# Splitting the first loads of a fused mean, matmul and residual kernel over three DMA queues

## The chip, the core and the metric

The kernel runs on one core of one Trainium2 chip. Its time is the device time of one execution in microseconds (us); lower is better. A core has TensorE (PE; its weight loads are shown as PEld), VectorE (DVE), ScalarE (ACT), GpSimd (POOL) and SyncE (SP), each with an instruction stream of its own that it works off in order, and 16 DMA engines that move data between the chip's main memory and the on-chip memory. A transfer is started by an instruction in the stream of SP, ACT or POOL; we call the transfers that one engine starts that engine's queue.

## The reference

Cut to what is computed (x is 4 x 1024 x 512, cond_512 is 4 x 256, W is 1536 x 512, b has 512 elements, all float32):

```python
hidden = jnp.concatenate([cond_512, cond_512], axis=-1)
x_mean = jnp.mean(x, axis=1, keepdims=True)
fused = jnp.concatenate([x, x_mean * ones_L, hidden[:, None, :] * ones_L], axis=-1)
out = x + jax.nn.relu(jnp.einsum('bld,do->blo', fused, W) + b)
```

The last two thirds of `fused` are the same for all 1024 positions of a row, so the kernel computes them once for each of the 4 rows as a bias: W's middle block times the mean of x, W's last block times cond (its two halves added first, since both halves of `hidden` are the same), plus b. What is left for every position is x times W's first block, plus that bias, then relu, then x is added again.

## The kernel before

**Tiles.** x is cut into 32 tiles `t` of 128 positions, 8 for each row. A tile's product needs x transposed, in 4 pieces `j` of 128 input columns, against `w_x[:, j]`, the rows of W's first block that belong to j. Float32 accuracy comes from a split: each operand is divided into a rounded part (`hi`, `w_hi`) and a remainder (`lo`, `w_lo`), and a product is three matmuls, hi by w_hi, hi by w_lo and lo by w_hi (`product`, line 576). So a tile is 12 matmuls of 128 x 512, and the 32 tiles are 384 of them.

**Steps for a piece.** `turn` (378) transposes: tiles 0 to 5 on TensorE by matmuls with an identity (389), later ones on VectorE from a second copy `z` of x that was loaded in another layout (391). `split_hi` (410) rounds on ScalarE, `split_lo` (429) subtracts, mostly on VectorE. Tiles 0 and 1 are turned whole, four transposes each; from tile 2 on, two tiles are turned together, one j at a time. The PSUM pool of the transposes has two buffers, so the turn of a piece waits until the `split_lo` of the piece two before it has read its buffer.

**The bias.** `fill` (396) transposes cond on TensorE (`pw`, from `c_sb`) and issues two matmuls on constants behind that. `turn_cond` (472) makes, on VectorE, `bL` from `b_sb` (473) and `cT` from `pw` (474); further steps on ScalarE, GpSimd and VectorE build `biases[r]`.

**Order.** The kernel does not write its order out by hand. `Plan` (20) holds every step with a cost on each engine that may do it, the steps it needs, and a due time. `simulate` and `run` try 1500 variations of the priorities with a fixed random seed, and the best simulated schedule is then emitted step by step. What an engine gets is therefore a fixed sequence. On the chip an engine waits at the head of its sequence until the data is there; nothing is reordered then. The times in the plan (`plan.done[...] = (at - HANDOVER, ...)`) are guesses that the planner takes for granted: when a load will have landed, or, with `later=3.0`, how long after its issue.

**The start, which the change touches.** Lines 226 to 244 run before the plan: a small activation that makes ScalarE load its function table (`table_warm`, 229), the identity, 9 matmuls on constants (`N_WARM`, 234), and on GpSimd the memsets of `b_sb` and of the mean matrix. Line 295 loads cond into `c_sb` over ScalarE's queue. Then lines 296 to 306 start seven loads, all over SyncE's queue in this order: x tile 0, x tile 1, W piece 0, W piece 1, W pieces 2 and 3, x tiles 2 and 3, x tiles 4 and 5. `load_mean` (319) follows; everything else is started by the plan. Two steps matter later: the load of `b_sb` (406) stands in ScalarE's sequence behind the rounding of the W pieces (it needs `("w_hi", J - 1)` in the plan), and `fill` (408) stands, in the plan, behind `("turn", 1)`, the transposes of tile 1:

```python
plan.add(("b",), {"act": 0.25}, [("w_hi", J - 1)], FIRST + 4, lambda e: nc.scalar.dma_start(
    out=b_sb[0:1, :], in_=b.rearrange("(o d) -> o d", o=1)), later=3.0)
plan.add(("fill",), {"pe": 0.22 * N_FILL + 0.2}, [("turn", 1)], 5.8, lambda e: fill())
```

Of the kernel before, what the change touches and what calls it, by code (L numbers as in the profile page):

```python
# [9 lines left out]
F32 = mybir.dt.float32  # L10
F32R = mybir.dt.float32r
BF16 = mybir.dt.bfloat16
AF = mybir.ActivationFunctionType
# [140 lines left out]
def kernel(  # L154
# [22 lines left out]
    nc = tc.nc  # L177
    B, L, D = x.shape
    H = cond.shape[1]
    P = 128  # L180
# [9 lines left out]
    N_FIRST = 1  # L190
# [12 lines left out]
    N_FILL = 2  # L203

    const = ctx.enter_context(tc.tile_pool(name="const", bufs=1))
# [11 lines left out]
    plan = Plan(["pe", "dve", "act", "pool", "sp", "aq"])  # L217
# [8 lines left out]
    warm = nc.const_aps.tensor(1.0, [P, 512], BF16)  # L226
    ones = const.tile([P, 1], F32, name="ones")
    nc.vector.memset(ones, 1.0)
    table_warm = const.tile([P, 1], F32, name="table_warm")
    nc.scalar.activation(table_warm, ones, AF.Relu)  # L230
    ident = const.tile([P, P], F32, name="ident")
    make_identity(nc, ident)
    pw = ps_b.tile([P, 512], F32, tag="b", name="pw")
# [4 lines left out]
    c_sb = const.tile([B, H], F32, name="c_sb")  # L238
# [28 lines left out]
    def load_x(e, g, i=0, n=G):  # L267
        r, k = divmod(g * G, NK)
        if not i:
            xs[g] = xpool.tile([P, G, D], F32, tag="x", name=f"x{g}")  # L270
        e.dma_start(out=xs[g][:, i : i + n], in_=xv[r, :, k + i : k + i + n, :])  # L271
# [17 lines left out]
    SP = 0.72  # L289
    SPZ2 = 1.85  # L290
    SPZ = 1.3
    def load_w(e, j, n):
        e.dma_start(out=w_x[:, j : j + n, :], in_=Wv[0, :, j : j + n])  # L293

    nc.scalar.dma_start(out=c_sb, in_=cond)
    for key, at, e, load in (
        (("x", 0, 0), 4.4, nc.sync, lambda e: load_x(e, 0, 0, 1)),
        (("x", 0, 1), 5.0, nc.sync, lambda e: load_x(e, 0, 1, 1)),
        (("w", 0), 5.8, nc.sync, lambda e: load_w(e, 0, 1)),
        (("w", 1), 7.0, nc.sync, lambda e: load_w(e, 1, 1)),  # L300
        (("w", 2), 8.4, nc.sync, lambda e: load_w(e, 2, 2)),
        (("x", 0, 2), 9.7, nc.sync, lambda e: load_x(e, 0, 2, 2)),
        (("x", 1, 0), 11.0, nc.sync, lambda e: load_x(e, 1, 0, 2)),
    ):
        load(e)
        plan.done[key] = (at - plan.HANDOVER, 0.0, "sp")
    w_cond = xpool.tile([P, 2, KH, D], F32, tag="x", name="w_cond")

    def load_cond():
        nc.sync.dma_start(  # L310
            out=w_cond, in_=W[2 * D : 3 * D].rearrange("(s h p) o -> p s h o", p=P, h=KH)
        )
# [3 lines left out]
    def load_mean(j, n):  # L316
        nc.sync.dma_start(out=w_mean[:, j : j + n, :], in_=Wv[1, :, j : j + n])

    load_mean(0, N_FIRST) if N_FIRST else None
    plan.free["sp"] = 8.9 + SP * N_FIRST  # L320
    plan.add("cond", {"sp": 4 * SP}, [], 13, lambda e: load_cond(), later=2.5)
    plan.add("w_mean", {"sp": (J - N_FIRST) * SP}, ["cond"], 14,
             lambda e: load_mean(N_FIRST, J - N_FIRST), later=2.5)
# [72 lines left out]
    def fill():  # L396
        for h in range(KH):
            nc.tensor.transpose(
                pw[:, h * B : (h + 1) * B], c_sb[:, h * P : (h + 1) * P], ident[:B, :B]
            )  # L400
        for _ in range(N_FILL):
            nc.tensor.matmul(
                pw[:, KH * B :], lhsT=warm[:, :P], rhs=warm[:, KH * B :], start=True, stop=True
            )

    plan.add(("b",), {"act": 0.25}, [("w_hi", J - 1)], FIRST + 4, lambda e: nc.scalar.dma_start(
        out=b_sb[0:1, :], in_=b.rearrange("(o d) -> o d", o=1)), later=3.0)
    plan.add(("fill",), {"pe": 0.22 * N_FILL + 0.2}, [("turn", 1)], 5.8, lambda e: fill())

    def split_hi(c):  # L410
        u, js = pieces[c]
# [24 lines left out]
    for c, (u, js) in enumerate(pieces):  # L436
# [12 lines left out]
        w = n * len(js)  # L449
# [273 lines left out]
```

## Time and profile before

| what | us |
|---|---|
| median of 8 executions | 108.86 |
| lowest and highest | 107.76, 109.85 |
| the profiled execution | 108.40 |
| span of the profile, first to last instruction | 106.6 |
| outside the span in that execution (108.40 - 106.6) | 1.8 |

All of the profile's times are counted from the span's start. The engines' busy times over the span:

```profile
PE 101.3 (95%) x443; PEld 79.6 (75%) x443; DVE 77.3 (73%) x118; ACT 57.6 (54%) x136; POOL 75.8 (71%) x68
```

TensorE is the busiest; its granted clock is given as 1.000 for the whole span. The 40 slices of 2.67 us show the DMA engines busy nearly throughout, and how much they moved at the start:

```profile
DMA  3999999999999999999999999999963399516552
GB/s 70 214 291 399 263 346 230 257 195 198 197 198 224 192 216 315 264 264 305 378 236 345 295 324 265 275 276 400 395 243 127 126 347 400 209 39 251 201 216 80
```

A digit is the busy share in tenths (9 is 90% or more); below it stands what was moved. The list of transfers, with the size of each and the median time from the issue to the landing (only the groups of the start):

```profile
x<-in_x_dram SPq DMA_DIRECT2D x2, 256.0 KB, 2.8
w_x<-in_L_cond_W_dram SPq DMA_DIRECT2D x2, 256.0 KB, 5.4
w_x<-in_L_cond_W_dram SPq DMA_DIRECT2D x1, 512.0 KB, 6.4
```

The first line is x tiles 0 and 1, the others are W's three loads. In these lists the suffix q (SPq, ACTq) stands for the engine's sequencer, which issues transfers and waits for semaphores while the engine itself may be busy with something else.

### The profile page before, as it was taken

Reading aid. Unit: us, or ns where it says so; the run is one execution under the profiler, and the core shown is the slowest. Engines: PE = TensorE matmul, PEld = TensorE weight load, DVE = VectorE, ACT = ScalarE, POOL = GpSimd, SP = SyncE. Lnnn points to the kernel's source line nnn. Section 1 sums busy time; section 2 is a strip of 40 time slices with the busy share of each in tenths; the row PEclk is TensorE's granted clock in tenths of the full one; section 3 lists DMA queues with packets and bytes.
Section 4 is the critical chain, followed back from the end, with each engine's and each line's share of the span. In section 5 each row is a group of like instructions: output and inputs, shape, how many; then the busy total and the mean of one; then the engine's idle time right before and its main releaser. Section 6 shows DMA issues by size and latency. Waiting matters only on the chain.

```text
span 106.6 us, 1462 instructions
## 1 busy us (share of the span) xinstructions
PE 101.3 (95%) x443; PEld 79.6 (75%) x443; DVE 77.3 (73%) x118; ACT 57.6 (54%) x136; POOL 75.8 (71%) x68
## 2 busy tenths in 40 slices
PE   7999959999999999999999999999999999999980
PEld 2547738887888878878888787888878878888870
DVE  0049643492899998999889699997998793481760
ACT  5053536595786996946597656436685520470000
POOL 5008206374499899999999989999979999099000
DMA  3999999999999999999999999999963399516552
GB/s 70 214 291 399 263 346 230 257 195 198 197 198 224 192 216 315 264 264 305 378 236 345 295 324 265 275 276 400 395 243 127 126 347 400 209 39 251 201 216 80
DMA packets 24049, 26.83 MB, mean 252 GB/s; under 512 B 1253, under 2 KB 14825, under 8 KB 24042
## 3 DMA queue, kind: packets, MB, share of 16 engines
q1 hardware_dynamic: 24032, 26.74, 92.2%
q8 instruction: 3, 0.05, 0.2%
q14 instruction: 4, 0.03, 0.1%
q10 hardware_dynamic: 10, 0.01, 0.0%
HBM read 18.36 MB, written 8.39 MB: 251 GB/s over the span
## 4 chain that ended last, share of the span: by engine, by line
PE 82%; DMA 11%; SPq 2%; DVE 1%; issue 0%; ACT 0%; DVEq 0%
PE po_None L595 77%; DMA w_x<-in_L_cond_W_dram 6%; DMA b_sb<-in_L_cond_b_dram 5%; PE po L595 3%; PE pb L521 2%; PE xT L389 1%; SPq L293 1%; SPq L271 1%; DVE bL L473 0%; DVE o L626 0%; DVE lo L432 0%; PE po L590 0%; DVE cT L474 0%; ACT w_hi L359 0%; DVEq L473 0%
## 5 line engine op out<-in xcount | busy, mean ns | idle before, releaser
L595 PE MATMUL po_None<-w_hi,hi 128*128 128x512 f32 x124 | 49.4, 400 | 0.2 <-DVE w_hi L360 0.2
L595 PE MATMUL po_None<-w_lo,hi 128*128 128x512 f32 x124 | 49.3, 399 | 0.0
L595 PE MATMUL po_None<-w_hi,lo 128*128 128x512 f32 x124 | 49.3, 399 | 0.0
L621 POOL TENSOR_TENSOR o<-o,x 128x512 f32<-128x512 f32 x28 | 35.7, 1302 | 4.2 <-ACT o L618 4.2
L416 ACT ACTIVATE hi<-xT 128x512 fp32r<-128x512 f32 (+1 forms) x38 | 20.3, 534 | 15.0 <-PE xT L389 9.8
L391 DVE STREAM_TRANSPOSE xT<-z 128x512 f32<-128x512 f32 (+1 forms) x28 | 28.1, 1031 | 0.3
L595 PEld LDWEIGHTS po_None<-w_lo,hi 128*128 128x128 f32 x124 | 23.3, 189 | 6.0 <-DVE w_lo L362 0.7
L595 PEld LDWEIGHTS po_None<-w_hi,hi 128*128 128x128 f32 x124 | 23.3, 189 | 5.9 <-ACT hi L416 0.7
L595 PEld LDWEIGHTS po_None<-w_hi,lo 128*128 128x128 f32 x124 | 23.4, 188 | 5.8 <-DVE lo L432 0.3
L432 DVE TENSOR_TENSOR lo<-xT,hi 128x512 fp32r<-128x512 f32 (+1 forms) x29 | 16.0, 575 | 4.3 <-ACT hi L416 4.3
L618 ACT ACTIVATE o<-o 128x512 f32<-128x512 f32 x28 | 16.8, 628 | 3.4 <-DVE o L613 2.5
L613 DVE TENSOR_TENSOR o<-po_None,bias 128x512 f32<-128x512 f32 x18 | 11.6, 679 | 6.1 <-issue 3.1
L613 POOL TENSOR_TENSOR o<-o,bias 128x512 f32<-128x512 f32 x10 | 13.0, 1311 | 0.5 <-ACT bias L527 0.5
L496 DVE SCALAR_TENSOR_TENSOR acc<-w_mean,tot,acc 128x512 f32<-128x512 f32 x15 | 11.3, 754 | 2.7 <-ACT acc L490 2.2
L432 POOL TENSOR_TENSOR lo<-xT,hi 128x512 fp32r<-128x512 f32 (+1 forms) x9 | 11.3, 1253 | 0.0
L507 POOL TENSOR_TENSOR cond<-bL,term 128x512 f32<-128x512 f32 x4 | 5.2, 1297 | 5.3 <-ACT term L502 5.3
L608 ACT ACTIVATE o<-po_None 128x512 f32<-128x512 f32 x10 | 5.9, 596 | 4.1 <-PE po_None L595 4.0
L362 POOL TENSOR_TENSOR w_lo<-w_x,w_hi 128x512 fp32r<-128x512 f32 x2 | 2.8, 1426 | 6.2 <-ACT w_hi L359 6.2
L416 ACT ACTIVATION_READ_ACCUMULATOR hi<-xT 128x1 f32 x36 | 7.0, 195 | 0.0
L527 ACT ACTIVATE bias<-pb 128x512 f32<-128x512 f32 x4 | 2.4, 598 | 8.2 <-PE pb L521 8.2
L389 PEld LDWEIGHTS xT<-ident,x 128*128 128x128 f32 x24 | 4.8, 209 | 2.7 <-DVE lo L432 1.7
L479 POOL TENSOR_TENSOR wc<-w_cond 128x512 f32<-128x512 f32 x2 | 2.5, 1292 | 5.7 <-DMA w_cond<-in_L_cond_W_dram 5.7
(52 smaller groups left out, 62.9 us busy)
## 6 DMA issues: line engine op xcount, KB each, us to landing
out_dram<-o SPq DMA_DIRECT2D x31, 256.0 KB, 4.0
z<-in_x_dram SPq DMA_DIRECT2D x24, 256.0 KB, 8.9
x<-in_x_dram SPq DMA_DIRECT2D x6, 1024.0 KB, 9.3
x<-in_x_dram SPq DMA_DIRECT2D x3, 512.0 KB, 8.2
w_cond<-in_L_cond_W_dram SPq DMA_DIRECT2D x1, 1024.0 KB, 10.0
w_mean<-in_L_cond_W_dram SPq DMA_DIRECT2D x1, 768.0 KB, 10.0
x<-in_x_dram SPq DMA_DIRECT2D x2, 256.0 KB, 2.8
w_x<-in_L_cond_W_dram SPq DMA_DIRECT2D x2, 256.0 KB, 5.4
```

Source lines behind the costliest of these rows:

```text
L362: lambda e, j=j: nc_of[e].tensor_tensor(w_lo[:, j, :], w_x[:, j, :], w_hi[:, j, :].bitcast(F32), ALU.subtract))
L389: nc.tensor.transpose(v[:, (m * n + i) * P : (m * n + i + 1) * P], x_t[:, j], ident)
L391: nc.vector.transpose(v[:, : n * P].rearrange("p (n t) -> p n t", t=Q), zs[u].rearrange("p n (a j) -> p n j a", j=J)[:, : n * NQ, js[0], :],)
L416: nc.scalar.activation(hi[c][:, :m], xT[c][:, :m], AF.Copy, accum_out=sums[:, r, js[0], s : s + 1] if len(js) == 1 else None,)
L432: nc_of[e].tensor_tensor(lo[c][:, :m], xT[c][:, :m], hi[c][:, :m].bitcast(F32), ALU.subtract)
L496: nc.vector.scalar_tensor_tensor(acc[r], w_mean[:, j, :], totals[r][:, j : j + 1], acc[r], ALU.mult, ALU.add)
L507: nc.gpsimd.tensor_tensor(conds[r], conds[r] if k else bL, terms[r, k], ALU.add)
L595: nc.tensor.matmul(pos[key][:, :w], lhsT=v[p][:, c], rhs=m[:, j, d], start=(not h and todo[key] == 3 * J), stop=(todo[key] == 1),)
L608: nc.scalar.activation(o_tile(t), pos[t], AF.Copy)
L613: nc_of[e].tensor_tensor(v if t >= ALONE else o_tile(t), v, biases[t // NK][:, d], ALU.add)
L618: nc.scalar.activation(outs[t], outs[t], AF.Relu)
L621: nc.gpsimd.tensor_tensor(outs[t], outs[t], x_tile(t), ALU.add)
```

## The change

The seven loads of the start keep their sizes and their helpers. The three of W go over ScalarE's queue instead of SyncE's, those of x stay on SyncE's, and the program now names them in turn. cond's load goes over GpSimd's queue; in the program it stands behind GpSimd's memsets. The activation that loads ScalarE's table stands behind the loads. In the plan, the guessed landing times change, SyncE is taken to be free at 7.8 instead of 8.9, and `fill` (cond's two transposes and the two matmuls behind them) needs only tile 0's transposes, not tile 1's. No computation is added or taken away. Since the planner works with these numbers, the order it emits for the rest of the kernel may differ as well.

```diff
@@ -226,8 +226,6 @@
     warm = nc.const_aps.tensor(1.0, [P, 512], BF16)
     ones = const.tile([P, 1], F32, name="ones")
     nc.vector.memset(ones, 1.0)
-    table_warm = const.tile([P, 1], F32, name="table_warm")
-    nc.scalar.activation(table_warm, ones, AF.Relu)
     ident = const.tile([P, P], F32, name="ident")
     make_identity(nc, ident)
     pw = ps_b.tile([P, 512], F32, tag="b", name="pw")
@@ -292,18 +290,21 @@
     def load_w(e, j, n):
         e.dma_start(out=w_x[:, j : j + n, :], in_=Wv[0, :, j : j + n])
 
-    nc.scalar.dma_start(out=c_sb, in_=cond)
+
     for key, at, e, load in (
-        (("x", 0, 0), 4.4, nc.sync, lambda e: load_x(e, 0, 0, 1)),
-        (("x", 0, 1), 5.0, nc.sync, lambda e: load_x(e, 0, 1, 1)),
-        (("w", 0), 5.8, nc.sync, lambda e: load_w(e, 0, 1)),
-        (("w", 1), 7.0, nc.sync, lambda e: load_w(e, 1, 1)),
-        (("w", 2), 8.4, nc.sync, lambda e: load_w(e, 2, 2)),
-        (("x", 0, 2), 9.7, nc.sync, lambda e: load_x(e, 0, 2, 2)),
-        (("x", 1, 0), 11.0, nc.sync, lambda e: load_x(e, 1, 0, 2)),
+        (("x", 0, 0), 4.8, nc.sync, lambda e: load_x(e, 0, 0, 1)),
+        (("w", 0), 5.1, nc.scalar, lambda e: load_w(e, 0, 1)),
+        (("x", 0, 1), 6.0, nc.sync, lambda e: load_x(e, 0, 1, 1)),
+        (("w", 1), 6.2, nc.scalar, lambda e: load_w(e, 1, 1)),
+        (("x", 0, 2), 8.3, nc.sync, lambda e: load_x(e, 0, 2, 2)),
+        (("w", 2), 8.0, nc.scalar, lambda e: load_w(e, 2, 2)),
+        (("x", 1, 0), 9.7, nc.sync, lambda e: load_x(e, 1, 0, 2)),
     ):
         load(e)
         plan.done[key] = (at - plan.HANDOVER, 0.0, "sp")
+    nc.gpsimd.dma_start(out=c_sb, in_=cond)
+    table_warm = const.tile([P, 1], F32, name="table_warm")
+    nc.scalar.activation(table_warm, ones, AF.Relu)
     w_cond = xpool.tile([P, 2, KH, D], F32, tag="x", name="w_cond")
 
     def load_cond():
@@ -317,7 +318,7 @@
         nc.sync.dma_start(out=w_mean[:, j : j + n, :], in_=Wv[1, :, j : j + n])
 
     load_mean(0, N_FIRST) if N_FIRST else None
-    plan.free["sp"] = 8.9 + SP * N_FIRST
+    plan.free["sp"] = 7.8 + SP * N_FIRST
     plan.add("cond", {"sp": 4 * SP}, [], 13, lambda e: load_cond(), later=2.5)
     plan.add("w_mean", {"sp": (J - N_FIRST) * SP}, ["cond"], 14,
              lambda e: load_mean(N_FIRST, J - N_FIRST), later=2.5)
@@ -405,7 +406,7 @@
 
     plan.add(("b",), {"act": 0.25}, [("w_hi", J - 1)], FIRST + 4, lambda e: nc.scalar.dma_start(
         out=b_sb[0:1, :], in_=b.rearrange("(o d) -> o d", o=1)), later=3.0)
-    plan.add(("fill",), {"pe": 0.22 * N_FILL + 0.2}, [("turn", 1)], 5.8, lambda e: fill())
+    plan.add(("fill",), {"pe": 0.22 * N_FILL + 0.2}, [("turn", 0)], 5.8, lambda e: fill())
 
     def split_hi(c):
         u, js = pieces[c]
```

## The prediction

> **What bounds the kernel now.** I read the page first: TensorE is busy for 95% of the span. Then I cut the span where TensorE's timeline has gaps and asked for each engine's busy time in the stretches. Columns: stretch, length, then busy time (and instructions) of PE, PEld, DVE, ACT, POOL, then granted clock, DMA share, GB/s.
>
> ```profile
> 4.50:7.42 2.92, 2.69 (x14) 1.88 (x12) 0.55 (x2) 1.19 (x2) 0.00 (x0) 1.00 0.87 222
> 7.42:9.00 1.58, 1.58 (x6) 0.87 (x7) 1.58 (x3) 0.63 (x2) 0.57 (x1) 1.00 1.00 386
> 9.00:14.47 5.47, 5.47 (x27) 4.08 (x25) 3.49 (x7) 2.70 (x10) 2.27 (x2) 1.00 1.06 329
> 14.47:15.76 1.29, 0.01 (x1) 0.01 (x1) 0.89 (x4) 0.30 (x1) 0.00 (x0) 1.00 1.06 346
> 15.76:103.60 87.84, 87.83 (x391) 71.35 (x391) 70.23 (x102) 51.30 (x121) 71.35 (x57) 1.00 0.95 255
> ```
>
> The reader is to see that from 15.76 to 103.60 TensorE never stops (87.83 of 87.84). The change takes no matmul away, so it can only move the moment at which that stretch starts, or put gaps into it. What can be had lies before: 0.23 idle before 7.42, 1.29 at 14.47, and a little between matmuls that count as busy (from 7.42 to 9.00 six matmuls fill 1.58; at the 0.233 of the later stretch, where 391 instructions include shorter ones, six take 1.40, so 0.2, and I count 0.3 with the next one). Together 1.8.
>
> Next, the chain of work that ended last (start, duration, what), for the gap at 14.47:
>
> ```profile
> 2.57 6.41 DMA w_x<-in_L_cond_W_dram
> ...
> 9.06 5.70 DMA b_sb<-in_L_cond_b_dram
> ...
> 15.37 0.34 DVE lo L432
> ...
> 15.76 0.51 PE xT L389 x2
> ```
>
> W's last load, issued at 2.57, lands at 8.97; only then does ScalarE pass its rounding of that piece and issue b's load, which takes 5.70; VectorE waits for b at `bL`, and a `lo` that TensorE's next transposes wait for is queued behind it. VectorE's own timeline shows that queue:
>
> ```profile
> 11.74 0.74 DVE L432 TENSOR_TENSOR lo<-xT,hi 128x256 fp32r<-128x256 f32 x2
> 14.87 0.43 DVE L473 TENSOR_SCALAR bL<-b_sb 128x512 f32<-128x512 f32 x1 [2.38 <-DMA b_sb<-in_L_cond_b_dram]
> 15.21 0.16 DVE L474 TENSOR_SCALAR cT<-pw 128x8 f32<-128x8 f32 x1
> 15.28 0.75 DVE L432 TENSOR_TENSOR lo<-xT,hi 128x256 fp32r<-128x256 f32 x2
> ```
>
> VectorE stands for 2.38 and TensorE, with work left for half of that, for 1.29. So not W's first piece but W's last piece, through b, sets the end. TensorE's timeline says what the first piece is worth:
>
> ```profile
> 4.50 1.91 PE L389 MATMUL xT<-ident,x 128*128 128x128 f32 x8
> 6.35 0.31 PE L398 MATMUL pw<-ident,c_sb 4*128 4x4 f32 x2
> 6.59 0.60 PE L402 MATMUL pw<-const-bfloat16-1.0 128*128 128x504 bf16 x2
> 7.42 0.71 PE L595 MATMUL po_None<-w_hi,hi 128*128 128x512 f32 x2 [0.23 <-DVE w_hi L360]
> ```
>
> The transposes of tiles 0 and 1 and `fill` occupy TensorE from 4.50 to 7.19. W's first piece holds it up for 0.23 only. Last, the DMA engines by the microsecond:
>
> ```profile
> 3.00:4.00 1.00, 1.00 (x4) 0.30 (x2) 0.00 (x0) 0.00 (x0) 0.00 (x0) 1.00 1.00 285
> 4.00:5.00 1.00, 1.00 (x5) 0.73 (x4) 0.00 (x0) 0.00 (x0) 0.00 (x0) 1.00 0.90 107
> 5.00:6.00 1.00, 1.00 (x7) 1.00 (x5) 0.00 (x0) 0.40 (x1) 0.00 (x0) 1.00 0.75 119
> 6.00:7.00 1.00, 1.00 (x6) 0.35 (x5) 0.16 (x1) 0.74 (x2) 0.00 (x0) 1.00 1.01 320
> ```
>
> They are 90% and 75% busy while they move 107 and 119 GB/s, against 386 from 7.42 on. That dip, when W's first rows are read, loses 2 x (1 - 113/386) = 1.4 us of transfer.
>
> **Part by part.** Differences are taken in the profiled execution (108.40: span 106.6 and 1.8 outside) and added to the median 108.86, which is 0.46 above it. I count the 1.8 outside as unchanged.
>
> *W on ScalarE's queue.* An issue takes 0.42 to 0.46 on SyncE (three in 1.37). First in ScalarE's sequence, W's loads are issued at about 0.73, 1.2 and 1.65 instead of 1.63, 2.09 and 2.57: 0.9 earlier each. But the first piece is worth at most 0.23 at 7.42, and an earlier w_hi and w_lo up to 0.3 between the first matmuls: -0.5 at best. For the last piece, which counts, both ends: if the dip runs beside x's loads instead of behind them, -1.4. If the queues share evenly, x tiles 2 and 3 (512 KB), which came after W, now come beside it, at 389 GB/s (the stretch from 8 to 9 us) +1.35. I take the middle, 0, since nothing in this trace shows two loaded queues at once. Here a rule of the Trainium skill speaks against the change. The row: with one queue the DMA engines are already 0.75 to 1.01 busy from 2 us on. DMA: Bandwidth & Descriptors, section "Issuing engines are not separate DMA queues", says that transfers started from several engines interleave on the same 16 DMA engines and that only issue time is saved. By it alone the sum would take the +1.35 end, less at most the 0.9 of issue; by the dip in the row, up to -1.4.
>
> *x.* Tiles 0 and 1 landed 2.8 after their issues, by 4.0; tile 0's transposes start at 4.50, when the 9 warm-up matmuls end (0.77 + 3.94, the last one's tail overlapped). Shared with W's first piece, tile 0 lands between 3.5 (as now) and 5.4 (4.0 for both pieces' 512 KB, plus the whole dip). Beyond 4.4 it costs TensorE directly: 0 to +1.0; I take +0.3, as the first half-microsecond of reading is x's as well as W's. Tile 1 may come up to 1 us later; `fill`, moved ahead of its transposes, covers 0.84 of that (6.35 to 7.19). Without that cover it would be added to the +0.3. TensorE's own path to 14.47 thus moves by -0.5 + 0.3 = -0.2, between -0.5 and +0.5.
>
> *The wait at b.* b's load is still issued behind ScalarE's rounding of W's last piece. Its 5.70 has bounds 2.8 (x's first loads) and 10.0 (`w_cond`, the longest in the list); its own row is the nearest, so 5.70. Then b lands where W's last piece puts it, VectorE's queue behind `bL` waits, and TensorE's 0.2 is swallowed there unless the planner puts another `lo` in front of `bL`. It may: the plan has x tiles 2 and 3 at 8.3 instead of 9.7 and W's first two pieces 0.7 to 0.8 earlier. One `lo` (about 0.4) more ahead of `bL` frees the next transposes. From none to the whole 1.29; I take 0.2 for the order, since the plan also moves b's own due landing ahead, by 0.4 with W's last piece.
>
> *cond on GpSimd's queue.* It stands behind memsets that end at 2.26 (1.97 + 0.29). Landing 1.7 (the fastest transfer of the list) to 5.7 (b) later: 4.0 to 8.0. TensorE needs it after tile 0's transposes, at about 5.5 (4.50 + 0.96); it used it at 6.35 before. With the 2.8 of x's loads, which ran beside the same start, it is there at 5.1: cost 0, under tile 0's transposes. At 8.0, the stall is +2.5 for everything queued behind on TensorE, tile 1's transposes first. GpSimd's next work is at 8.43, so nothing there waits for the issue.
>
> *Table load.* 1.28 plus 0.20, now from about 2.1 to 3.6; ScalarE is idle until 5.60. Cost 0; without this cover 1.5 at the first `hi`.
>
> *SyncE's other issues.* x tiles 2 to 5, `w_mean` and the first `z` leave 1.4 earlier; what they bring is first missed after 9 us. The wait for `w_cond` (GpSimd, until 16.93) has long slack before the first bias at 34.5. Cost 0 while that holds.
>
> Sum: -0.2 (order before `bL`) + 0 (W's last piece) + 0 (cond, table, SyncE) = -0.2, and 108.86 - 0.2 = 108.7.
>
> **The rivals.** *Faster: the wait at b goes.* The redrawn order puts enough `lo` ahead of `bL`, or W's last piece lands over 1 us earlier. For it: the dip of 1.4, and a plan in which x is 1.4 earlier. Against: b stays behind W. Then TensorE's -0.2 counts and the 1.29 is saved: 107.4; with every term at its best, -1.8, 107.0.
>
> *Slower: W's last piece lands later.* Place: ScalarE's rounding of it, b's issue behind, `bL` on VectorE. Price +1.35, 110.2. It decides from a landing of 10.1 on (8.97 + 1.1), if `bL` still has a `lo` behind it. For it: DMA engines that are full with one queue. Against: the dip may be hidden.
>
> *Slower: cond lands late.* `fill` ends at 8.84 instead of about 6.3, tile 1's transposes (0.96) at 9.8, the first product 2.4 later than 7.42; 1.29 of it falls into the gap at 14.47: +1.1, 110.0.
>
> *Slower: the redrawn order has a new stall.* In the 87.84 after 15.76 only 0.01 is idle, so a redraw can only lose there; one more wait like the present one is +1.3, 110.2.
>
> *No effect, because W comes no earlier:* that is the likeliest case with all terms at 0, 108.9.
>
> **How the numbers follow.** A measurement of this kernel (8 runs within 1% of the median) can't tell less than 1%, 1.09 us, from no change. Likeliest, little net: 0.38, its own range 107.8 to 109.8. The wait at b goes: 0.26. W's last piece late: 0.20. cond late: 0.08. A new stall: 0.08. So faster 0.26, same 0.38, slower 0.36. The range 107.2 to 110.4 takes in the cases at their prices and leaves out the last of each: some 0.08 below, 0.10 above.
>
> **What would show it.** In the changed profile: W's first piece landing before 6.8, but the first product no earlier than about 7.1; W's last load landing near 9, b's about 5.7 after its issue; VectorE waiting at L473 and TensorE behind it near 15. I am wrong if TensorE has no idle stretch between 9 and 17 us (then faster), if that stretch is over 2 us, if cond's transposes start after 6.5, or if TensorE idles after 17 us.

## The result, and the profile after

| | before | after |
|---|---|---|
| median (executions) | 108.87 (32) | 111.02 (11) |
| lowest and highest | 107.66, 110.13 | 110.84, 111.91 |
| the profiled execution | 108.40 | 110.87 |
| its span | 106.6 | 109.1 |
| TensorE's first product starts, last matmul ends | 7.42, 103.61 | 10.82, 105.94 |

The changed kernel is slower: after / before is 1.0243, with a 95% interval of 1.0208 to 1.0277. That is 2.3 us over the forecast and 0.6 us above the range. (Ratios here and below leave disturbed executions out, so one can differ from the quotient of two medians.)

The stretches of the prediction, cut where TensorE's timeline of the changed kernel changes; columns as there:

```profile
4.50:7.42 2.92, 1.31 (x5) 0.73 (x4) 0.84 (x2) 0.60 (x1) 0.00 (x0) 1.00 0.92 340
7.42:9.00 1.58, 0.01 (x1) 0.02 (x1) 1.47 (x3) 0.63 (x1) 0.34 (x1) 1.00 1.03 403
9.00:11.00 2.00, 2.00 (x9) 1.52 (x10) 0.00 (x0) 0.00 (x0) 0.92 (x1) 1.00 1.06 385
11.00:13.00 2.00, 2.00 (x6) 1.61 (x6) 1.17 (x2) 1.11 (x2) 0.61 (x1) 1.00 1.07 212
13.00:15.76 2.76, 2.76 (x15) 2.29 (x15) 2.49 (x4) 0.86 (x4) 0.68 (x1) 1.00 1.08 304
22.00:105.95 83.95, 83.93 (x373) 67.97 (x371) 68.23 (x98) 48.72 (x113) 68.94 (x55) 1.00 0.88 249
```

Before 9.00 TensorE is mostly idle (1.32 busy of 4.50), where it was nearly full. From 9.00 on it never stops: the gap of 1.29 behind b is gone. But read the counts too: from 11.00 to 13.00 only 6 instructions fill 2.00 us, from 13.00 to 15.76 15 fill 2.76. The first are slow, and the column of the granted clock says 1.00 all the same (what that column leaves out comes with e4). TensorE's timeline (start, duration, what, idle before and its releaser) shows both:

```profile
5.49 1.10 PE L390 MATMUL xT<-ident,x 128*128 128x128 f32 x4 [0.77 <-DMA x<-in_x_dram]
8.99 0.37 PE L399 MATMUL pw<-ident,c_sb 4*128 4x4 f32 x2 [2.40 <-DMA c_sb<-in_cond_dram]
9.29 1.02 PE L403 MATMUL pw<-const-bfloat16-1.0 128*128 128x504 bf16 x2
10.11 1.06 PE L390 MATMUL xT<-ident,x 128*128 128x128 f32 x4
10.82 0.77 PE L596 MATMUL po_None<-w_hi,hi 128*128 128x512 f32 x1
11.39 0.63 PE L596 MATMUL po_None<-w_lo,hi 128*128 128x512 f32 x1
11.82 0.63 PE L596 MATMUL po_None<-w_hi,hi 128*128 128x512 f32 x1
12.24 0.99 PE L596 MATMUL po_None<-w_hi,lo 128*128 128x512 f32 x2
13.07 0.39 PE L596 MATMUL po_None<-w_hi,hi 128*128 128x512 f32 x1
```

(Line numbers are one higher than before from the moved activation on.) Tile 0's transposes wait 0.77 for x, cond's transposes wait 2.40 for cond, and all that is queued behind cond, tile 1's transposes first, waits with them. The first product starts 3.40 later than before. From 11.39 to 13.07 four products start 0.42 apart, against the 0.233 of the prediction: half the rate. The chain of work that ended last names one transfer where it named two before:

```profile
2.21 6.73 DMA c_sb<-in_cond_dram
...
8.99 0.37 PE pw L399 x2
...
11.17 3.00 PE po_None L596 x9
```

VectorE's line for b, at which it had waited 2.38, waits 0.15 now:

```profile
17.39 0.43 DVE L474 TENSOR_SCALAR bL<-b_sb 128x512 f32<-128x512 f32 x1 [0.15 <-DMA b_sb<-in_L_cond_b_dram]
```

The account, taken from the starts of the same product in both kernels (with as many transposes ahead of it), closes. Two starts of the kernel before and one of the changed kernel that are not shown yet:

```profile
8.99 0.39 PE L595 MATMUL po_None<-w_hi,hi 128*128 128x512 f32 x1
16.57 0.39 PE L595 MATMUL po_None<-w_lo,hi 128*128 128x512 f32 x1
```

```profile
18.91 0.39 PE L596 MATMUL po_None<-w_lo,hi 128*128 128x512 f32 x1
```

The first product starts 3.40 later. Of this 2.94 are waits (0.77 + 2.40, less the 0.23 for W's first piece before), and the rest is mostly the slow rate of the two matmuls on constants (1.02 against 0.60). The sixth starts 4.08 later (13.07 against 8.99): the first five steps took 2.25 against 1.57 before, so 0.68 more (1.1 more than five steps of 0.233). The 26th starts only 2.34 later (18.91 against 16.57), and 1.56 of what comes off lies between the 21st (17.43 against 13.53) and the 26th, where the kernel before has its wait at b. From there on the distance stays; TensorE's last matmul ends 2.33 later.

Where the loads landed (us from the span's start):

| load | before | after |
|---|---|---|
| x tile 0, tile 1 | 3.43, 4.07 | 5.35, 7.58 |
| W piece 0, piece 1, last | 6.82, 7.69, 8.97 | 6.52, 7.92, 10.24 |
| x tiles 2 and 3, 4 and 5 | 10.34, 11.75 | 10.6, 12.54 |
| cond | - | 8.94 |

Nearly all are late, though from 1.5 to 9.0 the DMA engines moved no less: 257 GB/s before, 281 after. The bytes come in another order.

### The profile page after: what moved, and what is told of

The parts are those of the page before. It is cut to its first block, busy times and chain, and to the rows that moved or that the text cites. A ratio compares the mean times of both kernels' runs of the same rounds, so it can differ in the third digit from the quotient of the medians.

```text
span 109.1 us, 1470 instructions
## 1 busy us (share of the span) xinstructions
PE 102.0 (93%) x443; PEld 80.6 (74%) x443; DVE 78.0 (71%) x118; ACT 57.3 (53%) x136; POOL 76.2 (70%) x69
## 4 chain that ended last, share of the span: by engine, by line
PE 89%; DMA 6%; POOL 1%; DVE 0%; issue 0%; POOLq 0%
PE po_None L596 81%; DMA c_sb<-in_cond_dram 6%; PE po L596 3%; PE xT L390 2%; PE pb L522 2%; PE pw L403 1%; POOL b_sb L238 0%; DVE o L627 0%; PE pw L399 0%; POOL ident masks.py:199 0%; PE po L591 0%; POOL mean L242 0%; POOL ident masks.py:197 0%; POOL mean L240 0%; POOLq masks.py:199 0%
## 5 line engine op out<-in xcount | busy, mean ns | idle before, releaser
L596 PE MATMUL po_None<-w_hi,hi 128*128 128x512 f32 x124 | 50.1, 404 | 0.0
L596 PEld LDWEIGHTS po_None<-w_hi,hi 128*128 128x128 f32 x124 | 23.8, 192 | 5.5
L433 DVE TENSOR_TENSOR lo<-xT,hi 128x512 fp32r<-128x512 f32 (+1 forms) x29 | 16.5, 578 | 6.5 <-ACT hi L417 6.5
L503 ACT ACTIVATE term<-wc,cT 128x512 f32<-128x512 f32 x8 | 5.7, 725 | 0.9 <-POOL cond L508 0.8
## 6 DMA issues: line engine op xcount, KB each, us to landing
w_mean<-in_L_cond_W_dram SPq DMA_DIRECT2D x1, 768.0 KB, 10.6
```

The source lines that it names most:

```text
L433: nc_of[e].tensor_tensor(lo[c][:, :m], xT[c][:, :m], hi[c][:, :m].bitcast(F32), ALU.subtract)
L503: nc.scalar.activation(terms[r, k], wc[:, k], AF.Copy, scale=cT[:, k, r : r + 1])
L596: nc.tensor.matmul(pos[key][:, :w], lhsT=v[p][:, c], rhs=m[:, j, d], start=(not h and todo[key] == 3 * J), stop=(todo[key] == 1),)
```

## The experiments

Two theories at first. **A**: cond's landing on GpSimd's queue is what costs, with the half rate behind the pause. **B**: the split of W and x over two queues costs, through W's pieces that land late. (Later letters refine these; their sentences say how.) An edit is shown against the kernel named. Ratios are to the kernel before on the same chip.

### cond alone

**e1**, after, with cond's load on ScalarE's queue ahead of W's:

```diff
+    nc.scalar.dma_start(out=c_sb, in_=cond)
...
-    nc.gpsimd.dma_start(out=c_sb, in_=cond)
```

> The changed kernel with cond's 4 KB load back on ScalarE's queue, ahead of W's three loads; the order of everything else is the same. Theory A (cond's late landing holds TensorE, and the pause halves its clock): cond has landed before 4 us, cond's transposes start right behind tile 0's, at about 6.5 instead of 8.99, the first product at about 8 instead of 10.82, and the time falls by 2 to 3 us to 108.0 to 109.0. Theory B (x shares the DMA engines with W and comes late; cond's wait only covers that): tile 0's transposes still start about 5.5, tile 1's late too, the first product not before 9.5, time 110 or more. Theory C (the order that the planner drew anew has its own stalls): no change beyond 0.5 us, 110.5 to 111.5.

Measured: 109.97 (4 executions), 1.0112 [1.0036, 1.0187], between the two theories (their ranges end at 109.0 and begin at 110). TensorE's timeline of this run:

```profile
7.50 0.47 PE L596 MATMUL po_None<-w_hi,hi 128*128 128x512 f32 x1 [1.34 <-DVE w_hi L361]
...
10.17 0.50 PE L596 MATMUL po_None<-w_hi,hi 128*128 128x512 f32 x1 [1.53 <-ACT w_hi L360]
```

The first product is back at 7.50, but the products now wait for W's pieces, 1.34 and 1.53; W's last load lands at 11.8. The stretches of the same run show what follows on the pauses:

```profile
7.50:10.57 3.07, 1.37 (x4) 0.71 (x5) 1.78 (x3) 1.08 (x2) 0.37 (x1) 1.00 1.03 406
10.57:13.99 3.42, 3.42 (x11) 2.66 (x10) 2.85 (x4) 0.99 (x4) 2.19 (x2) 0.50 1.08 234
13.99:20.00 6.01, 6.01 (x34) 5.16 (x33) 2.81 (x8) 3.05 (x13) 1.30 (x2) 1.00 1.11 242
```

The granted clock is 0.50 for 3.42 us, with 11 instructions in them; 34 fill the next 6.01. So there is a second late load beside cond. But e1 is not the change with cond's lateness taken out: W's loads now stand behind cond's and are issued 0.5 to 0.6 later, and with that x tiles 0 and 1 land earlier than in the change (3.43 and 5.38 against 5.35 and 7.58) and W's last load later (11.80 against 10.24). Between these two kernels half a microsecond of issue goes with which queue's loads come late.

**e2**, before, with cond alone on GpSimd's queue:

```diff
-    nc.scalar.dma_start(out=c_sb, in_=cond)
+    nc.gpsimd.dma_start(out=c_sb, in_=cond)
```

> The kernel before, with nothing but cond's load moved to GpSimd's queue; W and x stay together on SyncE's. If a small load over GpSimd's queue is slow by itself, it lands at about 8.9 as in the changed kernel (6.7 us after its issue), cond's transposes, here behind tile 1's, start at 9.0, the first product near 10, and the time is 110.5 to 111.5. If it was slow only because two other queues were loaded, it lands near 5, nothing waits, and the time is that of the kernel before, 108.5 to 109.2.

Measured: 108.75 (10), 0.9999 [0.9947, 1.0050]. Beside one loaded queue, cond lands 5.3 after its issue, at 7.56. TensorE and VectorE:

```profile
4.51 1.26 PE L389 MATMUL xT<-ident,x 128*128 128x128 f32 x8
7.60 0.28 PE L398 MATMUL pw<-ident,c_sb 4*128 4x4 f32 x2 [1.83 <-DMA c_sb<-in_cond_dram]
```

```profile
14.71 0.43 DVE L473 TENSOR_SCALAR bL<-b_sb 128x512 f32<-128x512 f32 x1 [0.28 <-DMA b_sb<-in_L_cond_b_dram]
```

TensorE loses 1.83 there, and its granted clock is 0.50 from 8.26 to 11.68; yet little is lost at the end, since the wait at b swallows it (0.28 is left of 2.38, and TensorE's idle 1.29 is gone): the 21st product starts 1.79 later than before, the 26th and all behind it 0.23. So cond's queue alone does not make the kernel slow. But here cond's transposes stand behind tile 1's; in the change they stand ahead of them (see e12).

**e3**, after, with `fill` behind tile 1 again:

```diff
-    plan.add(("fill",), {"pe": 0.22 * N_FILL + 0.2}, [("turn", 0)], 5.8, lambda e: fill())
+    plan.add(("fill",), {"pe": 0.22 * N_FILL + 0.2}, [("turn", 1)], 5.8, lambda e: fill())
```

> The changed kernel with cond's transposes behind tile 1's again. Theory A: tile 1's transposes run while cond is under way (6.6 to about 7.5), cond still lands near 8.9, the first product starts near 9.9 instead of 10.82, time 109.6 to 110.4. Theory B: no difference, since tile 1's x is late anyway, 110.7 to 111.3.

Measured: 110.44 (4), 1.0166 [1.0101, 1.0230]. The first product starts at 9.98; waits of 1.11 and 0.91 for x and 0.25 for cond take the place of the 2.40. x's tile 1 is itself late.

**e13**, after, with `fill` later still, so that cond can't be waited for:

```diff
-    plan.add(("fill",), {"pe": 0.22 * N_FILL + 0.2}, [("turn", 0)], 5.8, lambda e: fill())
+    plan.add(("fill",), {"pe": 0.22 * N_FILL + 0.2}, [("part", 1, J - 1, 2)], FIRST + 5, lambda e: fill())
-    plan.add(("turn_cond",), {"dve": 0.3}, [("fill",), ("b",)], FIRST + 5, lambda e: turn_cond())
+    plan.add(("turn_cond",), {"dve": 0.3}, [("fill",), ("b",)], FIRST + 7, lambda e: turn_cond())
```

> The changed kernel with cond's transposes put behind tile 1's products in the plan, so that cond's landing (near 8.9) is off TensorE's path; all loads and their queues are those of the change. If cond's wait and the pause it makes are the larger part of the loss, the ratio to before falls from 1.024 to 1.010 or less. If the split is the larger part, tile 1's transposes still wait for x (to about 7.6) and products for W's pieces, and the ratio stays at 1.015 or more.

Measured: 110.32 (6), 1.0194 [1.0137, 1.0252]. With cond out of TensorE's way, x and b are waited for:

```profile
6.26 2.13 PE L390 MATMUL xT<-ident,x 128*128 128x128 f32 x8 [1.55 <-DMA x<-in_x_dram]
```

```profile
17.90 0.43 DVE L474 TENSOR_SCALAR bL<-b_sb 128x512 f32<-128x512 f32 x1 [3.40 <-DMA b_sb<-in_L_cond_b_dram]
```

Behind `bL` TensorE waits 1.49 for a `lo` (at 18.79): the chain of the prediction, from W's last load (10.08 here) through b. So with cond off the path 1.9% of the 2.4% are left. The other 0.5% would be cond's share, but the two intervals overlap, so it can't be told from nothing.

### The half rate

**e4**, after, with six more matmuls on constants in `fill`, ahead of cond's transposes; they add nothing to the result:

```diff
+        for _ in range(6):
+            nc.tensor.matmul(
+                pw[:, KH * B :], lhsT=warm[:, :P], rhs=warm[:, KH * B :], start=True, stop=True
+            )
```

> The changed kernel with 6 more matmuls on constants (128 x 504, bfloat16) between tile 0's transposes and cond's, where TensorE waits for cond: 2.5 us at 0.42 each. It adds work to TensorE and takes no wait away. If the pause is what keeps TensorE at half speed until 13 us (5 products at 0.427 instead of 0.233, two matmuls on constants at 0.42 instead of 0.22), the products run at 0.233 from the first or second on, and the time falls by 0.8 to 1.4 us to 109.6 to 110.2, with cond's landing and the end of the wait unchanged. If the half speed has nothing to do with the pause, the time stays at 110.8 to 111.4 or grows.

Measured: 110.25 (4), 1.0157 [1.0083, 1.0231]. TensorE:

```profile
5.78 0.72 PE L390 MATMUL xT<-ident,x 128*128 128x128 f32 x4 [1.29 <-DMA x<-in_x_dram]
6.34 1.45 PE L399 MATMUL pw<-const-bfloat16-1.0 128*128 128x504 bf16 x6
...
9.10 0.28 PE L403 MATMUL pw<-ident,c_sb 4*128 4x4 f32 x2 [1.31 <-DMA c_sb<-in_cond_dram]
...
10.13 0.48 PE L600 MATMUL po_None<-w_hi,hi 128*128 128x512 f32 x1
10.45 0.39 PE L600 MATMUL po_None<-w_lo,hi 128*128 128x512 f32 x1
```

cond comes no earlier, but the pause is 1.31 instead of 2.40, and products follow at 0.23 from the second on (10.45, then 10.68). The median is 0.77 lower, though the intervals of the two ratios overlap. (The added lines shift the line numbers by four more.)

That the added work kept the rate up is not shown. In this execution the four transposes ahead of it already start 0.12 apart from the second on. In the changed kernel's profile the same four start 0.21 apart, ahead of any wait for cond (1.10 for four against 0.72 here), like those of the kernel before (1.91 for eight), whose matmuls on constants behind them are fast (0.60 for two). So there TensorE was at half rate before the pause and had not been at the full rate yet; the granted clock of the profile, 1.00, doesn't count this first slow stretch. e2 is the other case: transposes at 0.12 (1.26 for eight, the first two slow), a pause of 1.83, then the half rate, and the record shows it. Whether the pause in the changed kernel kept the half rate up stays open.

### The split

**e5**, before, with W's three loads on ScalarE's queue and named in turn with x's; plan, cond and `fill` as before:

```diff
+        (("w", 0), 5.8, nc.scalar, lambda e: load_w(e, 0, 1)),
         (("x", 0, 1), 5.0, nc.sync, lambda e: load_x(e, 0, 1, 1)),
-        (("w", 0), 5.8, nc.sync, lambda e: load_w(e, 0, 1)),
-        (("w", 1), 7.0, nc.sync, lambda e: load_w(e, 1, 1)),
-        (("w", 2), 8.4, nc.sync, lambda e: load_w(e, 2, 2)),
+        (("w", 1), 7.0, nc.scalar, lambda e: load_w(e, 1, 1)),
         (("x", 0, 2), 9.7, nc.sync, lambda e: load_x(e, 0, 2, 2)),
+        (("w", 2), 8.4, nc.scalar, lambda e: load_w(e, 2, 2)),
```

> The kernel before with W's three loads on ScalarE's queue and x's on SyncE's, named in turn; cond stays ahead of W's on ScalarE's queue, and all numbers of the plan, and so the order, are those of before. Theory A2 (the split itself makes W late, since x's later loads then run beside W's): W's last piece lands at 10.2 to 11.8 instead of 8.97, b's load, which stands behind its rounding, lands as much later, TensorE's wait near 15 grows from 1.3 to 2.5 or more, and the time is 110.0 to 111.5. Rival (the split does no harm, only cond's queue did): W's last piece lands near 9 and the time is 108.3 to 109.2.

Measured: 111.45 (6), 1.0329 [1.0247, 1.0412]: the split alone costs at least as much as the whole change (the intervals overlap). It is not quite the change's split: W stands behind cond's load here, and its last load lands later (12.17 against 10.24). The transfers (size, median time from issue to landing) and what TensorE waited for (sum, count, longest):

```profile
x<-in_x_dram SPq DMA_DIRECT2D x2, 256.0 KB, 2.9
w_x<-in_L_cond_W_dram ACTq DMA_DIRECT2D x2, 256.0 KB, 7.9
w_x<-in_L_cond_W_dram ACTq DMA_DIRECT2D x1, 512.0 KB, 9.8
```

```profile
PE po_None L595 <- DVE w_hi L360: 1.6, 1, 1.6
PE po_None L595 <- ACT w_hi L359: 1.2, 2, 1.0
PE xT L389 <- DVE lo L432: 1.0, 1, 1.0
```

x is as early as before; W, issued behind cond's load, takes 9.8 for its last load where it took 6.4, and lands at 12.17. The third line is the chain of the prediction: W's last piece, b, `bL`, the `lo` behind it.

**e6**, before, with only the plan's numbers of the change:

```diff
-        (("w", 2), 8.4, nc.sync, lambda e: load_w(e, 2, 2)),
+        (("w", 2), 8.0, nc.sync, lambda e: load_w(e, 2, 2)),
...
-    plan.free["sp"] = 8.9 + SP * N_FIRST
+    plan.free["sp"] = 7.8 + SP * N_FIRST
```

(the other landing times likewise, in the change's numbers, and `fill` needs tile 0 alone)

> The kernel before with only the plan's numbers of the change (guessed landing times, SyncE free at 7.8, cond's transposes behind tile 0's); the loads and their queues are those of before. If the newly drawn order has stalls of its own, the time is 110 or more. If it is as good as the old one, 108.2 to 109.2, and with more subtractions ahead of the wait for b, 107.4 to 108.2.

Measured: 108.10 (12), 1.0016 [0.9967, 1.0065]. No cost of the new order by itself can be seen.

**e12**, after, with W back on SyncE's queue in the old order; cond stays on GpSimd's, the plan stays:

```diff
-        (("w", 0), 5.1, nc.scalar, lambda e: load_w(e, 0, 1)),
+        (("w", 0), 5.1, nc.sync, lambda e: load_w(e, 0, 1)),
```

(the other two likewise, behind x tile 1; the table's activation as before)

> The changed kernel with W's loads back on SyncE's queue in the order of before; cond stays on GpSimd's queue and its transposes behind tile 0's. Theory A2+A: cond lands near 7.5, TensorE waits about 2 for it behind tile 0's transposes, tile 1's transposes come after, the first product near 9 and at half speed, the time 109.0 to 110.2, between the plan alone (108.1) and the whole change (111.0). Rival (cond's queue costs nothing without the split, as in the run where it alone was moved): 107.9 to 108.8.

Measured: 109.47 (6 executions, 107.12 to 110.83) beside 109.12, with no ratio. cond lands at 7.56 and TensorE waits 2.04 for it. Not telling by its time: it lies within the expected stretch, and also within the scatter of the kernel before. Its profile (110.21) speaks against leaving cond out of the account: with all of x and W on SyncE's queue, and W's last load at 9.01, the first product starts at 9.44, the next ones 0.43 apart, and TensorE's last matmul ends 1.66 later than in the profile of before. Unlike in e2, tile 1's transposes wait with cond's here, as in the change.

**e9**, before, the other way round: x tiles 0 and 1 on ScalarE's queue, W and the rest on SyncE's:

```diff
-        (("x", 0, 0), 4.4, nc.sync, lambda e: load_x(e, 0, 0, 1)),
+        (("x", 0, 0), 4.4, nc.scalar, lambda e: load_x(e, 0, 0, 1)),
```

(x tile 1 likewise)

> The kernel before with x tiles 0 and 1 on ScalarE's queue (behind cond) and W, then all later x, on SyncE's: two loaded queues at the start as in the change, but no later load of x runs beside W. Plan and order are those of before. Theory A2 (W is late because 1.5 MB of later loads share the DMA engines with it): W's last piece lands at 8.5 to 9.3, time 107.8 to 109.0. Rival (two loaded queues are slow in themselves, or W's reads are slow beside any other): W's last piece lands after 10 and the time is 110 or more.

Measured: 112.28 (6), 1.0323 [1.0272, 1.0374]. W lands at 4.25, 6.28 and 8.82, as expected, and the time is far off the expectation, because x is late now:

```profile
7.83 0.72 PE L389 MATMUL xT<-ident,x 128*128 128x128 f32 x4 [3.12 <-DMA x<-in_x_dram]
...
10.04 1.13 PE L389 MATMUL xT<-ident,x 128*128 128x128 f32 x4 [1.49 <-DMA x<-in_x_dram]
```

So W on the second queue is late in e5, and x on the second queue is late here. Either ScalarE's queue is the worse one, or whatever is on it shares the DMA engines with loads of SyncE's that are needed later. Two runs tell these apart.

**e15**, before, with all seven loads on ScalarE's queue; SyncE's next load is held until W's last piece is there, by a one-column copy into its target:

```diff
-        (("x", 0, 0), 4.4, nc.sync, lambda e: load_x(e, 0, 0, 1)),
+        (("x", 0, 0), 4.4, nc.scalar, lambda e: load_x(e, 0, 0, 1)),
...
+    nc.gpsimd.tensor_copy(w_mean[:, 0, 0:1], w_x[:, 3, 0:1])
```

> The kernel before with all seven loads on ScalarE's queue in the order of before, behind cond's, and SyncE's first load held until W's last piece has landed, so that ScalarE's queue runs alone at first. If a queue is as good as the other, the landings are those of before plus the later issue (0.5 to 0.9): W's last piece at 9.0 to 9.9, x tile 0 at 3.9 to 4.4. If ScalarE's queue is slow in itself, W's last piece lands after 11.

Measured: 108.57 (10), 1.0017 [0.9966, 1.0069]. Transfers:

```profile
x<-in_x_dram ACTq DMA_DIRECT2D x2, 256.0 KB, 2.9
w_x<-in_L_cond_W_dram ACTq DMA_DIRECT2D x2, 256.0 KB, 5.6
w_x<-in_L_cond_W_dram ACTq DMA_DIRECT2D x1, 512.0 KB, 6.4
```

2.9, 5.6 and 6.4 beside 2.8, 5.4 and 6.4 before: alone, ScalarE's queue is as good as SyncE's.

**e14**, e5 with everything from x tiles 2 and 3 on held in the same way:

```diff
+        if key == ("x", 0, 2):
+            nc.gpsimd.tensor_copy(xs[0][:, 2, 0:1], w_x[:, 3, 0:1])
```

> The kernel before with W on ScalarE's queue, as in the run with the split alone, but x tiles 2 and 3 (and all that follows on SyncE's queue) are held until W's last piece has landed, by a copy of one column of that piece into their buffer, which the load then overwrites. If W was late because later loads ran beside it, its last piece lands at 8.0 to 9.2 instead of 12.2, its second before 7.5 instead of 9.8. If ScalarE's queue is slow in itself, the last piece lands after 10. The time says little, since the held loads come later than before.

Measured: 110.81 (4, from 109.49 to 113.19), 1.0167 [1.0078, 1.0256]. As expected the time says little; the landings are what is read:

```profile
w_x<-in_L_cond_W_dram ACTq DMA_DIRECT2D x2, 256.0 KB, 3.9
w_x<-in_L_cond_W_dram ACTq DMA_DIRECT2D x1, 512.0 KB, 5.0
```

With nothing later beside them, W's loads land at 5.11, 6.09 and 7.32, where e5 had 12.17 for the last and the kernel before 8.97. This shows that sharing with later loads is what made W late. The held x comes at 10.81 and costs TensorE 1.6 there.

**e16** and **e17**, before, with both queues in order of need: x tiles 0 and 1, cond and b on SyncE's; W, then x tiles 2 to 5 on ScalarE's; SyncE's next load held. e17 also has earlier landing times in the plan:

```diff
-        (("w", 0), 5.8, nc.sync, lambda e: load_w(e, 0, 1)),
+        (("w", 0), 5.8, nc.scalar, lambda e: load_w(e, 0, 1)),
...
+    nc.sync.dma_start(out=c_sb, in_=cond)
+    nc.sync.dma_start(out=b_sb[0:1, :], in_=b.rearrange("(o d) -> o d", o=1))
+    nc.gpsimd.tensor_copy(w_mean[:, 0, 0:1], w_x[:, 3, 0:1])
```

(the other loads of W and x tiles 2 to 5 likewise; cond's old load goes, and the plan's step for b emits nothing)

> The kernel before with x tiles 0 and 1, cond and b on SyncE's queue, W and behind it x tiles 2 to 5 on ScalarE's, and SyncE's next load held until W's last piece has landed (a copy of one column of it into the buffer that this load overwrites). The order of everything else is that of before. If the split does harm only where later loads run beside W: W's last piece lands at 7 to 8, x tiles 2 and 3 by 10, the first product starts near 6, the wait for b is gone, and the time is 105.5 to 107.3. If two queues cost something beyond that: 108 or more.

> The same, with the plan's guessed landing times moved earlier by 0.3 (x tile 1) to 1.7 (W's last piece). If the planner's order matters for the gain, it is faster than the run before it by up to 0.7; if TensorE is already without gaps there, the same within 0.4.

Measured: 108.93 (12), 0.9967 [0.9879, 1.0056], and 108.83 (12), 0.9975 [0.9935, 1.0016]. A split that is closer to the order of need shows no cost, but the gain that I expected isn't there either (105.5 to 107.3; from 108 on the expectation says that two queues cost something beyond). x tile 1, on SyncE's queue but issued 0.25 behind W's first load on the other, lands at 7.00, where the kernel before had it at 4.07:

```profile
7.04 0.74 PE L391 MATMUL xT<-ident,x 128*128 128x128 f32 x4 [1.47 <-DMA x<-in_x_dram]
```

So a good part of what is won at b is lost there. In e16's profile (107.45) TensorE's last matmul still ends 0.94 earlier than before; its twelve executions reach from 107.10 to 110.47 and don't bear that out.

### b's load at the start

**e7**, before, with b's load issued behind cond's on ScalarE's queue:

```diff
     nc.scalar.dma_start(out=c_sb, in_=cond)
+    nc.scalar.dma_start(out=b_sb[0:1, :], in_=b.rearrange("(o d) -> o d", o=1))
...
-    plan.add(("b",), {"act": 0.25}, [("w_hi", J - 1)], FIRST + 4, lambda e: nc.scalar.dma_start(
-        out=b_sb[0:1, :], in_=b.rearrange("(o d) -> o d", o=1)), later=3.0)
+    plan.add(("b",), {"act": 0.25}, [("w_hi", J - 1)], FIRST + 4, lambda e: None, later=3.0)
```

> The kernel before with b's load issued at the start on ScalarE's queue, right behind cond's, instead of behind the rounding of W's last piece; the order of everything else is the same. If TensorE's wait of 1.29 at 14.47 comes from b alone, it is gone and the time is 107.3 to 107.9. If another wait stands right behind it, the time stays at 108.3 or more.

Measured: 0.9881 [0.9785, 0.9976]; its six executions reach from 106.53 to 110.96, with a median of 108.84, so one can't rely on it. The profiled one (106.56) shows the mechanism in its stretches:

```profile
14.47:15.76 1.29, 1.29 (x8) 1.12 (x7) 0.42 (x1) 1.09 (x4) 0.00 (x0) 1.00 1.15 208
```

The gap that TensorE had here is full, and its last matmul ends at 101.75 instead of 103.60.

**e11** is e6 with the same edit on b:

> The kernel before with the plan's numbers of the change and b's load at the start: all loads of x and W on SyncE's queue, cond and b on ScalarE's. If the wait for b is the one thing left at the start, 106.5 to 107.7; if W's second piece, for which TensorE waited 1.6 in the run with the plan alone, decides instead, 107.8 to 108.5.

**e10** is e7 with cond on GpSimd's queue:

```diff
-    nc.scalar.dma_start(out=c_sb, in_=cond)
+    nc.gpsimd.dma_start(out=c_sb, in_=cond)
     nc.scalar.dma_start(out=b_sb[0:1, :], in_=b.rearrange("(o d) -> o d", o=1))
```

> The kernel before with b's load at the start (ScalarE's queue) and cond's on GpSimd's. With cond's load alone moved the time did not change, though TensorE waited 1.8 for cond. Theory D (the wait for b near 15 swallowed it): with b early nothing swallows it, the first product starts near 8 and TensorE's last matmul 1.0 to 2.0 later than in the run with b early alone (101.5), and the fastest executions are 1.0 to 2.0 above that run's fastest (106.5), 107.5 to 108.5. Rival (a wait for cond ahead of the first product costs nothing, since W is not there yet): fastest near 106.5.

**e8** is after, with cond on ScalarE's queue ahead of W's loads and b behind them:

```diff
+    nc.scalar.dma_start(out=c_sb, in_=cond)
...
-    nc.gpsimd.dma_start(out=c_sb, in_=cond)
+    nc.scalar.dma_start(out=b_sb[0:1, :], in_=b.rearrange("(o d) -> o d", o=1))
```

> The changed kernel with cond's load back on ScalarE's queue, ahead of W's, and b's behind W's three at the start. Both small loads are then off TensorE's path, and what is left of the change is the split of W and x and the new order. Theory A2: W's second and third pieces land after 9 and near 11, TensorE waits for their rounding (1.5 in the run with cond alone moved back), and the time is 109.2 to 110.2. Rival (only the two small loads were late): 107.0 to 108.0.

Measured: e11 108.33 (12), 0.9947 [0.9911, 0.9983]; e10 108.04 (6, from 106.24 to 109.30), 0.9847 [0.9772, 0.9921]; e8 110.62 (6), 1.0238 [1.0169, 1.0307]. The intervals of e11 and e10 lie below 1: for e11 by half a per cent, with its profiled last matmul where before has it (103.6); for e10 from six executions that scatter by 3 us. A sure gain is not shown. In e10's profiled execution (109.04) cond costs TensorE a wait of 2.1 with nothing left to swallow it, but its fastest was expected no lower than 107.5 and took 106.24; whether cond on GpSimd's queue costs anything once b is early stays open. e8 leaves both small loads harmless and is as slow as the change: TensorE waits 1.6 for the rounding of W's second piece, W's last load lands at 11.59, and the half rate lasts 6.8 us.

## Why the prediction was wrong

**The step that failed** is the line of the sum "0 (W's last piece) + 0 (cond, table, SyncE)": two loads whose landing counts were charged nothing, though other loads now run beside them. In the changed kernel's profile the term that shows is cond, "It is there at 5.1: cost 0": it landed at 8.94, TensorE stood 2.40 for it, and the chain that ended last runs through it.

W's last load was the other, "I take the middle, 0, since nothing in this trace shows two loaded queues at once". It landed 1.27 later (10.24 against 8.97), near the bound of +1.35 that had been worked out for x tiles 2 and 3 coming beside it. In the changed kernel TensorE never stood for it (VectorE 0.15 at b), because TensorE was later still; with cond out of the way (e13) VectorE stands 3.40 at b and TensorE 1.49 behind. e14 against e5 shows the cause: W's last load lands at 12.17 with later loads beside it, at 7.32 without. A middle between two mechanisms was no estimate: the DMA engines were 90% and 75% busy in the dip, and I treated the dip's low GB/s as room that another queue could fill. The engines did move more (281 against 257 GB/s up to 9.0), but what they moved included loads that nobody waited for yet. The Trainium skill, DMA: Bandwidth & Descriptors, section "Issuing engines are not separate DMA queues", says that such transfers interleave on the same 16 engines; this trace and e5, e9, e14 and e15 agree, and going by it alone would have taken the right end. The price at that end, 110.2, is still 0.8 short: here cond and the slow rate stand ahead of it.

**x.** "Beyond 4.4 it costs TensorE directly": right, tile 0 landed at 5.35, inside 3.5 to 5.4, and cost 0.77 where I took 0.3. "Tile 1 may come up to 1 us later" was too little: 3.51 later. I let x share with W's first piece alone, not with W's next pieces as well; e3 shows the waits that follow when `fill` isn't in front.

**cond.** "It is there at 5.1: cost 0" failed, and so did its bounds: 6.73 after the issue, at 8.94, with 8.0 as the upper end. The rows I took had run beside one queue (e2: 5.3), this one ran beside two. The rival "cond lands late" had the mechanism: first product 9.8 at a landing of 8.0, hence 10.74 at 8.94, measured 10.82. Of the signs of being wrong that were named, "if cond's transposes start after 6.5" is the one that came with its cause (8.99).

**Rivals taken as exclusive.** Late cond (110.0) and W's late last load (110.2) were given 8% and 20% as if only one could happen. They came together: with two loaded queues cond took 6.7 instead of e2's 5.3, and W's last load 8.6 instead of 6.4. Nor do their costs add up, since each hides behind the other: late cond behind tile 1's transposes costs nothing (e2), the split alone 3.3% with W issued behind cond (e5), and without cond on the path 1.9% of 2.4% stay (e13). So the split is enough to make most of the loss. That the loss goes when the split alone is undone is not shown: e2 and e6 are each level with before, but e12, which joins them, is too scattered by its times, and its profile loses 1.66 to cond.

**Not priced: the half rate.** TensorE's pause was costed as its length. Behind it the products ran at half the rate until 13.07, 0.68 more than the same five steps took before. The half rate was there ahead of the pause already (e4's transposes against the changed kernel's), so it is part of the loss, but not shown to be an effect of the pause.

**What was right.** The wait at b as the cushion: e2 stands 1.83 for cond and ends level, within 0.5%, and the cushion went away here because TensorE itself came later. It was a little thicker than the 1.29 of the trace's idle time: 1.56 by the starts of the products around it, and the first five steps lost 0.40 where I counted 0.3 with the step behind them. I had written "I am wrong if TensorE has no idle stretch between 9 and 17 us (then faster)"; the bracket was wrong, since that stretch also closes when everything ahead of it moves back. W's first piece landed 0.3 earlier (6.52), before 6.8 as forecast, and to no use, as TensorE stood at cond then. The redrawn order brings no visible cost (e6), and the moved table load none: it ends at 3.64, and ScalarE's next work waits for TensorE until 6.62.

**Left open**: cond's own share beside the split (e13's and the change's intervals overlap, and e12 doesn't decide), whether the pause keeps TensorE at half rate in the changed kernel, and the wide scatter of the versions with b early.

## What to carry to other kernels

When the DMA engines are already nearly full, a second queue adds little transfer (281 against 257 GB/s here) and changes the order: work out for each load which later loads will now run beside it, and price the lateness of every one that is needed first, all of them together. Put a small load that an in-order engine will wait for ahead of the large ones, and look for the small load that is issued late without need, as b was (the wait for it goes in e7; how much time that saves is unsure). A pause of the bound engine costs its length and, on TensorE, sometimes a slow stretch behind it (e2 has one, e11 none), unless a wait further on swallows both.

## What the runs showed of the hardware

- Where the record shows the half rate in the first 20 us, it is one or two stretches of the same length, not a ramp: granted clock 0.50 from 10.57 to 13.99 (e1, pauses of 1.34 and 1.53), from 8.26 to 11.68 (e2, a pause of 1.83) and from 8.98 to 15.8 (e8): 3.42, 3.42 and 6.8 us. It does not follow every pause: e11 has one of 1.98, and its products behind it are at 0.23 again without a drop. The Trainium skill, TensorE: Matmul & The Clock Gate, Part 1, gives a free-running window of 3413 ns and 426.7 ns for a cold matmul of 512 columns; the 0.427 here agrees. It lets the clock drop after about a whole idle window; here a pause of 1.83 was enough in e2, and there the measurement decides.
- The granted clock of the profile can miss it: the changed kernel's profile says 1.00 from 9.00 to 13.00 while products start 0.427 apart. What it misses is the slow stretch at the start: in every run most of the nine warm-up matmuls start 0.42 apart, and the moment at which the fast rate comes differs between executions (the first transposes start 0.21 apart in the profile of before, 0.12 apart in e7's, which have the same work ahead of them).
- A small transfer is not a quick one beside loaded queues: cond's 4 KB took 5.3 us beside one (e2) and 6.7 beside two, b's 2 KB 5.70.
